# Reordering background work of a time-mix and GELU feed-forward kernel: copies first, an earlier first mix, weight terms in block 0

## The chip, the cores and the metric

One core of a Trainium2 chip. The metric is device time in microseconds, the median of repeated executions of the same program; lower is better.

## The reference

The input `x` is (4, 1024, 512) in f32. It is normalized over its last axis, goes through two branches, and both results are added to `x`.

```python
xn = _layernorm(x, axis=-1)
# attention-like branch, HIDDEN = 704
xx = concatenate([xn[:, 1:2], xn[:, :-1]], axis=1) - xn      # neighbour minus now
k = einsum('btc,hc->bth', xn + xx * time_mix_k, Wk)
r = einsum('btc,hc->bth', xn + xx * time_mix_r, Wr)
w = exp(-exp(time_decay))
state_t = state_{t-1} * w + relu(k_t);  out_t = state_t * r_t     # scan over the 1024 tokens
out = layernorm(einsum('bth,ch->btc', out, Wv)) * ln_gamma + ln_beta
# feed-forward branch, 2048 hidden
D = gelu(fp16(xn) @ W0.T + bias0).astype(fp16)
E = (D @ W1.T + bias1).astype(fp16)
return x + out + E
```

## The kernel before, in words

The tokens are cut into eight **blocks** of 512: `i` is the block at work, `j = i + 1` the next one. Even blocks begin a sequence, odd ones carry on from the state of the one before. All products run on TensorE in a reduced f32 format; for exactness operands are split into terms by VectorE and ScalarE. `split_x` makes three terms h, l, m of an x chunk, `split_kr` three terms of one tile of Wk or Wr (`kind` 0 is k, 1 is r), `split_w0`, `load_w1` and `split_wv` do so for the other weights. Terms that later blocks need are stored to DRAM (`krd`, `w0d`, `w1d`) and loaded from there (`load_kr`, `load_w1`, `load_w0l`).

A block is a loop over 16 **chunks** `n` of the feed-forward's hidden axis. In a chunk TensorE runs 8 matmuls of the up product (`up`, line 786, for the chunk two ahead), 8 of the down product (`down`, line 808, four accumulators `pe`, one for each 128 tokens) and then one **piece** of the attention branch: `raw_k`, `raw_r` and `raw_halves` in block 0 (plain f32 weights), `three_pass` (lines 628 and 385) and `half_pass` in later blocks, `out_full`/`out_halves` or `out_three_pass` (lines 723 to 733) in chunks 12 to 15. A normal chunk with a three-pass piece has 28 matmuls, one with a piece of the output 33.

A piece returns a **follower**, a generator with the work that ScalarE and VectorE do on its result in the next chunk: a scaled copy of `pa` on ScalarE (line 640, for the output 737), VectorE's combination with `pb` (641, 738), then the scan, the gating or the normalization with the residual (`residual`, lines 705 to 716, where two GpSimd instructions at lines 299 and 300 make the reciprocal deviation). Beside it runs the chunk's **background** list `bg[n]`, filled by `put`: loading, normalizing and transposing the next block's x (`turn`, line 331), its fp16 copies (`x16`), the scaled copies `scaled_now` (line 351), `mixed` (365 and 369) with the split of xk, and in the first two blocks the weight splits. `woven` alternates one step of each follower with one step of the background list. The order on TensorE, VectorE, ScalarE and the SP queue is exactly the order in which this code issues.

At the end of a block `rounded` empties the four `pe` banks on VectorE (line 765); the next block's down product takes the same four banks. Other buffers: four banks "mm" for all other products, six scratch tiles "s" (`temp`), six tiles "kr" (two weight tiles of three terms), two "w1", and 62 tiles "q" for everything that lives longer, raw weights among them. In block 0 the raw r weights are read by `raw_r` and stay in "q" until block 1 splits them.

In block 0, followers are finished at once, and `load_w1` for the chunk two ahead splits raw weights at the end of a chunk, after the background list; `store_weights` then issues the stores that the chunk has gathered on SP.

Of the kernel before, what the change touches and what calls it, by code (L numbers as in the profile page):

```python
# [22 lines left out]
def time_mix_and_gelu_ffn(  # L23
# [257 lines left out]
    def split_x(raw, name):  # L281
        u = truncated(raw, f"u{name}")
        h, l, m = (part(f"{p}{name}") for p in "hlm")
        nc.scalar.copy(h, u)  # L284
        yield
        nc.vector.tensor_sub(l, raw, u)
        yield
        nc.vector.scalar_tensor_tensor(m, l.bitcast(F32), -S, u, ALU.mult, ALU.add)
        return h, l, m
# [65 lines left out]
    def mixed(i, c):  # L355
        t0 = blocks[i][1]
        prior, now = xnT[:, c, :TB], xnT[:, c, 1:]
        if t0 > 0:
            nc.gpsimd.tensor_copy(xnT[:, c, 0:1], last[:, c, :])
        else:  # L360
            nc.vector.tensor_copy(xnT[:, c, 0:1], now[:, 0:2][:, 1:2])
        if t0 + TB < T:
            nc.gpsimd.tensor_copy(last[:, c, :], xnT[:, c, TB : TB + 1])
        xk, xr = parts_now.pop((i, c))
        nc.vector.scalar_tensor_tensor(
            xk, prior, mk_sb[:, c : c + 1], xk, ALU.mult, ALU.add
        )
        yield
        nc.vector.scalar_tensor_tensor(  # L369
            prior, prior, mr_sb[:, c : c + 1], xr, ALU.mult, ALU.add  # L370
        )
        xks[i, c] = yield from split_x(xk, f"k_{i}_{c}")
        xrs[i, c] = prior

    def split_xr(i, c):
        xrs[i, c] = yield from split_x(xrs[i, c], f"r_{i}_{c}")
# [127 lines left out]
    def woven(works, jobs):  # L504
        def steps():
            for job in jobs:
                yield from job() or ()
                yield

        others = steps()  # L510
        while works:
            works = [w for w in works if next(w, works) is None]
            next(others, None)
        finished(others)


# [187 lines left out]
    def residual(i, s, po):  # L704
        mv = small([P, 1, 2], "mv1", f"mvy_{i}_{s}", 4)
        stats_of(mv, 0, po, f"sty_{i}_{s}")
        rstd = rstd_of(mv[:, :, 1], f"ry_{i}_{s}")
        z = zs[i][:, s, :]
        y = temp(f"o_{i}_{s}") if i < RAW_OUT else po
        nc.vector.scalar_tensor_tensor(  # L710
            y, po, mv[:, 0, 0:1], gamma_sb, ALU.subtract, ALU.mult
        )

        yield
        nc.vector.scalar_tensor_tensor(y, y, rstd, beta_sb, ALU.mult, ALU.add)  # L715
        nc.vector.tensor_add(z, z, y)
# [152 lines left out]
    with tc.manual_schedule(engines=engines):  # L869
        for i in range(len(blocks)):  # L870
# [6 lines left out]
                bg[n].append(lambda: fn(*args))  # L877

            def fetch_kr(block, kind, h):
                if block == 1 and kind == 1:  # L880
                    ks[block, kind, h] = split_kr(kind, h)
                else:
                    ks[block, kind, h] = load_kr(block, kind, h)

            def fetch_x():
                state["x"] = load_x(j, "x")
# [12 lines left out]
            if i == 0:  # L899
                state["x"] = x_next  # L900
                pieces[1, 0] = [raw_k, i, 3]
                pieces[3, 0] = [raw_r, i, 3]
                pieces[5, 0] = [raw_k, i, 4]
                pieces[7, 0] = [raw_r, i, 4]
                pieces[9, 0] = [
                    lambda i: raw_halves(i, [bank(f"pkr_{i}_{q}") for q in range(2)]), i
                ]
                put(0, several, split_w0, (1, 2), (1, 3))
                for c in range(NC):
                    put(2 + c - (c == 0), split_w0, 2, c)  # L910
                    put(3 + c, load_w0, 3, c)
                    put(5 + c, split_w0, 3, c)
                put(1, stats, *range(NS))
                put(3, lambda: norm_apply(j, state["x"]))
                for h in range(NF):
                    put(1 + 2 * h, split_kr, 0, h)
                put(4, turn, 0, 1)
                put(5, turn, 1, 5)
                put(7, turn, 5, 10)
                put(8, turn, 10, 11)  # L920
                put(9, turn, 11, 16)
                put(4, load_late_constants)
                put(12, split_half)
                mix_at = (11, 12, 13, 15)
            else:
                order = [(0, h) for h in range(NF)] + [(1, h) for h in range(NF)]
                for k, (kind, h) in enumerate(order):
                    pieces[k + 2 * kind, 0] = [three_pass, i, kind, h]
                    if k > 1:
                        first = (5, 6, 8, 9, 10)[h] if i == kind == 1 else k - 2 + 2 * (k > 6)  # L930
                        put(first, fetch_kr, i, kind, h)
                pieces[5, 0] = [half_pass, i, 0]
                pieces[6, 0] = [half_pass, i, 1]
                for c, n in enumerate((1, 2, 3, 4) if i == 1 else (2, 2, 3, 3)):
                    put(n, split_xr, i, c)
                if j <= LAST:
                    put(2, fetch_x)
                    for s in range(NS):
                        put(4 + s // 2 if i == 1 else 4, stats, s)
                    put(6 if i == 1 else 5, lambda: norm_apply(j, state["x"]))  # L940
                    turns = (0, 5, 5, 5, 1) if i == 1 else (3, 4, 4, 3, 2)
                    for k in range(sum(turns)):
                        unit = next(n for n in range(5) if k < sum(turns[: n + 1]))
                        put(6 + unit, turn, k, k + 1)
                mix_at = (12, 13, 15, 15) if i == 1 else (12, 13, 14, 15)
            if i == 1:
                for g in range(NN // G):
                    put(2 * g, store_w0l, g)
                for h, n in enumerate((7, 10, 11, 12, 13, 13)):
                    put(n, split_wv, h)  # L950
            put(11 if j <= LAST else 2, fetch_residual)
            if j <= LAST:
                for c in range(NC):
                    put((10 if i == 0 else 11) + c // 2, x16, j, c)
                for c, n in enumerate(mix_at):
                    if n == mix_at[c - 1]:
                        put(n, scaled_now, j, c)
                    else:
                        early[n].append((j, c))
                    put(n, mixed, j, c)  # L960
                put(13, fetch_kr, j, 0, 0)
                put(14, fetch_kr, j, 0, 1)

            pe = [ps_e.tile([P, C], F32, tag="pe", name=f"pe_{i}_{s}") for s in range(NS)]
            for n in range(NN):
                ahead = n + AHEAD
                if ahead == NN and j <= LAST:
                    xf = next_xf
                nxt = (i, ahead) if ahead < NN else (j, ahead - NN)
                gelu = up(*nxt) if nxt[0] <= LAST else None  # L970
                several(scaled_now, *early[n])
                works = [follow() for follow in followers]
                if i == 0 or n == NN - NS or (n > NN - NS and i < RAW_OUT):
                    finished(*works)
                    works = []
                else:
                    works = [w for w in works if next(w, works) is None]
                followers = []
                if gelu:
                    d = gelu()  # L980
                if ahead + 1 == NN and j <= LAST:
                    next_xf = ffn_input(j)
                if n < NN - tail:
                    operands = waiting.pop(0)
                    for s in range(NS):
                        down(n, s, *operands, end=NN - tail if s in by_columns else NN)
                if gelu and i > 0:
                    waiting.append((d, load_w1(*nxt)))
                two_on = (i, ahead + 2) if ahead + 2 < NN else (j, ahead + 2 - NN)
                if two_on[0] <= LAST:  # L990
                    load_w0l(*two_on)
                jobs = [
                    lambda s=s: finish(i - 1, s, e16s[s])
                    for s in (2 * n, 2 * n + 1)
                    if s < len(e16s)
                ]
                for s in range(NS):
                    if (n, s) in pieces:
                        fn, *args = pieces[n, s]
                        followers.append(fn(*args))  # L1000
                if i == 0 and ahead + 1 < NN:
                    load_w1_raw(ahead + 1)
                woven(works, jobs + bg[n])
                if i == 0:
                    waiting.append((d, load_w1(*nxt)))
                store_weights()
# [60 lines left out]
```

## Time and profile before

| | us |
|---|---|
| median of 3 runs (889.73 to 890.12) | 889.89 |
| the profiled execution | 890.49 |
| its span, first to last instruction | 888.7 |
| TensorE busy | 867.3 (98%) |
| VectorE busy | 674.6 (76%) |
| ScalarE busy | 429.2 (48%) |
| GpSimd busy | 81.4 (9%) |
| moved by DMA | 195.01 MB, 219 GB/s on average |

Instructions are given as start, duration, engine, line of the source, operation and tiles out<-in. In brackets stands the engine's idle time before the instruction, and what ended it. Times are counted from the span's start. In the profile PE is TensorE, DVE VectorE, ACT ScalarE, POOL GpSimd, SP the queue that issues DMAs.

Blocks begin on TensorE at about 40, 136, 249, 355, 461, 568, 674 and 780 us.

### The profile page before, as it was taken

What the parts mean: (1) busy time and instruction counts of PE and PEld (TensorE: products, weight loads), DVE (VectorE), ACT (ScalarE), POOL (GpSimd) and SP (SyncE); (2) the same over time, 40 slices, a digit from 0 to 9 for tenths busy, and PEclk for the clock granted to TensorE, in tenths of its full rate; (3) what the DMA queues carried; (4) which work ended last, traced back from release to release, by engine and by line L of the source; (5) the groups of instructions that cost most, each with busy time, mean ns of one, the idle gap of its engine ahead of it and who ended that gap; (6) DMA issues with size and microseconds to landing.
All of it is one profiled execution on the core that took longest, in us unless ns stands there. A gap on an engine that the chain in (4) does not pass through costs nothing.

```text
span 888.7 us, 11076 instructions
## 1 busy us (share of the span) xinstructions
PE 867.3 (98%) x3760; PEld 687.3 (77%) x3760; DVE 674.6 (76%) x1098; ACT 429.2 (48%) x733; POOL 81.4 (9%) x142
## 2 busy tenths in 40 slices
PE   8999999999999999999999999999999999999996
PEld 7676658777578887888878888788887888878885
DVE  4767867598887878878788777878788786884547
ACT  3855734346634365443635446344463445444430
POOL 1100000000011001000021001100011200200001
PEclk8999999999999999999999999999999999999999
DMA  9569746866458655876548666595654956558631
GB/s 264 199 232 333 244 162 224 282 213 217 162 198 303 222 181 177 276 246 240 178 146 317 224 211 201 170 343 199 224 188 159 342 197 224 178 193 299 241 120 48
DMA packets 100164, 195.01 MB, mean 219 GB/s; under 512 B 10991, under 2 KB 25356, under 8 KB 100108
## 3 DMA queue, kind: packets, MB, share of 16 engines
q1 hardware_dynamic: 100048, 194.29, 64.0%
q8 instruction: 30, 0.49, 0.2%
q14 instruction: 26, 0.21, 0.1%
q10 hardware_dynamic: 60, 0.02, 0.0%
HBM read 165.43 MB, written 28.84 MB: 219 GB/s over the span
## 4 chain that ended last, share of the span: by engine, by line
PE 80%; DVE 11%; ACT 4%; POOL 2%; issue 2%; DVEq 0%; ACTq 0%
PE pd L786 22%; PE pe L808 22%; PE pa L628 13%; PE pb L385 7%; PE po L684 4%; PE oa L723 3%; PE ph L657 2%; PE pk L385 2%; PE pr L385 2%; PE ob L731 1%; POOL ry L300 1%; DVE oy L715 1%; DVE xnT L369 1%; DVE sty L305 1%; POOL ry L299 1%
## 5 line engine op out<-in xcount | busy, mean ns | idle before, releaser
L808 PE MATMUL pe<-w,d 128*128 128x512 f32 x1008 | 251.7, 392 | 6.6 <-DVE e L765 6.6
L808 PEld LDWEIGHTS pe<-w,d 128*128 128x128 f32 x1008 | 187.6, 188 | 51.2 <-DVE e L765 13.2
L786 PE MATMUL pd<-xf,w0h 128*128 128x512 f32 x512 | 204.4, 399 | 0.7 <-DVE y L641 0.7
L786 PE MATMUL pd<-xf,w0l 128*128 128x512 f32 x512 | 200.0, 391 | 0.0
L796 ACT ACTIVATE d<-pd,late_sb 128x512 f16<-128x512 f32 x128 | 87.7, 685 | 120.5 <-PE pd L786 120.2
L786 PEld LDWEIGHTS pd<-xf,w0h 128*128 128x128 f32 x512 | 96.7, 189 | 27.2 <-issue 5.7
L786 PEld LDWEIGHTS pd<-xf,w0l 128*128 128x128 f32 x512 | 96.6, 189 | 21.9 <-issue 1.9
L641 DVE SCALAR_TENSOR_TENSOR y<-pb,a 128x512 f32<-128x512 f32 x70 | 48.3, 690 | 63.8 <-PE pb L385 43.3
L640 ACT ACTIVATE a<-pa 128x512 f32<-128x512 f32 x70 | 41.8, 597 | 86.4 <-PE pa L628 86.4
L801 ACT CAST d<-d 128x512 fp32r<-128x512 f16 x128 | 79.5, 621 | 4.1
L331 DVE STREAM_TRANSPOSE xnT<-x 32x512 f32<-32x512 f32 x112 | 78.6, 702 | 2.0
L299 POOL TENSOR_SCALAR ry<-mvy 128x1 f32<-128x1 f32 x32 | 19.8, 619 | 431.2 <-DVE mvy L306 431.2
L628 PE MATMUL pa<-hk,kr 128*128 128x512 f32 x140 | 54.5, 389 | 0.0
L628 PE MATMUL pa<-lk,kr 128*128 128x512 f32 x140 | 54.5, 389 | 0.0
L643 ACT ACTIVATE y<-y 128x512 f32<-128x512 f32 x35 | 22.1, 633 | 57.7 <-DVE y L641 57.7
L628 PE MATMUL pa<-hr,kr 128*128 128x512 f32 x120 | 46.7, 389 | 0.0
L628 PE MATMUL pa<-lr,kr 128*128 128x512 f32 x120 | 46.7, 389 | 0.0
L723 PE MATMUL oa<-wv,hg 128*128 128x512 f32 x120 | 46.7, 389 | 0.0
L723 PE MATMUL oa<-wv,lg 128*128 128x512 f32 x120 | 46.7, 389 | 0.0
L284 ACT CAST hk<-uk 128x512 fp32r<-128x512 f32 x28 | 17.4, 621 | 56.9 <-DVE uk L235 56.9
L385 PE MATMUL pb<-mk,kr 128*128 128x512 f32 x140 | 37.4, 389 | 0.0
L521 DVE TENSOR_TENSOR_SCAN g<-late_sb,carry,y 128x512 f32<-128x512 f32 x20 | 25.7, 1284 | 14.1 <-ACT y L643 14.1
(166 smaller groups left out, 1359.6 us busy)
## 6 DMA issues: line engine op xcount, KB each, us to landing
w<-w1d SPq DMA_DIRECT2D x110, 512.0 KB, 3.6
kr<-krd SPq DMA_DIRECT2D x195, 256.0 KB, 4.9
w0l<-w0d SPq DMA_DIRECT2D x96, 256.0 KB, 4.1
x<-in_L_attn_x SPq DMA_DIRECT2D x32, 256.0 KB, 6.0
w1d<-w SPq DMA_DIRECT2D x16, 512.0 KB, 3.4
xres<-in_L_attn_x SPq DMA_DIRECT2D x32, 256.0 KB, 5.4
krd<-wt SPq DMA_DIRECT2D x30, 256.0 KB, 2.4
out<-xres SPq DMA_DIRECT2D x28, 256.0 KB, 3.9
```

The lines of the kernel that those rows point to most:

```text
L299: nc.gpsimd.tensor_scalar_add(r, var, EPS)
L331: nc.vector.transpose(dst[i * Q : (i + 1) * Q, :, :, j, :], src[j * Q : (j + 1) * Q, :, :, i, :],)
L385: return nc.tensor.matmul(dst, w[:, c, :], src, start=(c == 0), stop=(c == NC - 1))
L628: nc.tensor.matmul(pa, w[p][:, c, :], xs[j, c][p], start=(c == 0 and p == 0), stop=(c == NC - 1 and p == 1),)
L640: nc.scalar.activation(a, pa, AF.Copy, scale=1.0 + 1.0 / S)
L641: nc.vector.scalar_tensor_tensor(y, pb, -1.0 / S, a, ALU.mult, ALU.add)
L684: nc.tensor.matmul(pos[s], gs[i, h][:, s * P : (s + 1) * P], wv_raw[h], start=(h == 0), stop=False,)
L723: nc.tensor.matmul(pa, gs[i, h][p][:, cols], wv[h][p], start=(h == 0 and p == 0), stop=(h == NF - 1 and p == 1),)
L786: nc.tensor.matmul(pd, w, xf[c], start=(c == 0 and p == 0), stop=(c == NC - 1 and p == 1),)
L796: nc.scalar.activation(d16, pd, AF.Gelu, bias=b0_sb[:, n : n + 1])
L801: nc.scalar.copy(d, d16)
L808: nc.tensor.matmul(pe[s] if sum_ is None else sum_, d[:, s * P : (s + 1) * P], w1[p][:, cols], start=(n == first and p == 0), stop=(n == e ...
```

## The change

It has four parts, all of them of order:

- In a chunk, the first step of each follower, which holds the ScalarE copy of the piece, is issued ahead of `scaled_now` instead of behind it. `woven` starts with a background step instead of a follower's. `residual` has one more `yield` from block 2 on, after the GpSimd instructions.
- The split of xk leaves `mixed` and becomes a job of its own, `split_xk`. From block 1 on the first x chunk is mixed in chunk 10 and split in 11; the others follow in 12, 13, 15 (block 1) or 12, 13, 14. Transposes end with chunk 9 instead of 10, and `x16` begins in chunk 10. No two mixes share a chunk any more.
- `split_kr` for the r weights runs in block 0 (chunks 1, 3, 5, 7, 11), and block 1 loads those terms from DRAM in chunks 3, 4, 7, 8, 9, as later blocks do.
- In block 1 `split_xr` is one chunk later (2 to 5), and the first of the `split_wv` are moved from 7 and 10 to 9 and 11.

```diff
-        xks[i, c] = yield from split_x(xk, f"k_{i}_{c}")
-        xrs[i, c] = prior
+        xks[i, c], xrs[i, c] = xk, prior
+
+    def split_xk(i, c):
+        xks[i, c] = yield from split_x(xks[i, c], f"k_{i}_{c}")
...
         while works:
+            next(others, None)
             works = [w for w in works if next(w, works) is None]
-            next(others, None)
...
         rstd = rstd_of(mv[:, :, 1], f"ry_{i}_{s}")
+        if i >= RAW_OUT:
+            yield
...
             def fetch_kr(block, kind, h):
-                if block == 1 and kind == 1:
-                    ks[block, kind, h] = split_kr(kind, h)
-                else:
-                    ks[block, kind, h] = load_kr(block, kind, h)
+                ks[block, kind, h] = load_kr(block, kind, h)
...
                     put(1 + 2 * h, split_kr, 0, h)
+                    put((1, 3, 5, 7, 11)[h], split_kr, 1, h)
...
-                        first = (5, 6, 8, 9, 10)[h] if i == kind == 1 else k - 2 + 2 * (k > 6)
-                        put(first, fetch_kr, i, kind, h)
+                        put(k - 2 + 2 * (k > 6), fetch_kr, i, kind, h)
...
-                for c, n in enumerate((1, 2, 3, 4) if i == 1 else (2, 2, 3, 3)):
+                for c, n in enumerate((2, 3, 4, 5) if i == 1 else (2, 2, 3, 3)):
                     put(n, split_xr, i, c)
...
-                    turns = (0, 5, 5, 5, 1) if i == 1 else (3, 4, 4, 3, 2)
+                    turns = (1, 6, 6, 3) if i == 1 else (4, 5, 4, 3)
...
-                mix_at = (12, 13, 15, 15) if i == 1 else (12, 13, 14, 15)
+                mix_at = (10, 12, 13, 15) if i == 1 else (10, 12, 13, 14)
...
-                for h, n in enumerate((7, 10, 11, 12, 13, 13)):
+                for h, n in enumerate((9, 11, 11, 12, 13, 13)):
                     put(n, split_wv, h)
...
-                    put((10 if i == 0 else 11) + c // 2, x16, j, c)
+                    put((10, 10, 11, 12)[c], x16, j, c)
                 for c, n in enumerate(mix_at):
-                    if n == mix_at[c - 1]:
-                        put(n, scaled_now, j, c)
-                    else:
-                        early[n].append((j, c))
+                    early[n].append((j, c))
                     put(n, mixed, j, c)
+                    put(n + (n == 10), split_xk, j, c)
...
+                works = [follow() for follow in followers]
+                works = [w for w in works if next(w, works) is None]
                 several(scaled_now, *early[n])
-                works = [follow() for follow in followers]
                 if i == 0 or n == NN - NS or (n > NN - NS and i < RAW_OUT):
                     finished(*works)
                     works = []
-                else:
-                    works = [w for w in works if next(w, works) is None]
```

More of the change, by code (lines that the diff above doesn't have):

```diff
@@ L940, in time_mix_and_gelu_ffn @@
                     put(6 if i == 1 else 5, lambda: norm_apply(j, state["x"]))
-                    turns = (0, 5, 5, 5, 1) if i == 1 else (3, 4, 4, 3, 2)
+                    turns = (1, 6, 6, 3) if i == 1 else (4, 5, 4, 3)
                     for k in range(sum(turns)):
-                        unit = next(n for n in range(5) if k < sum(turns[: n + 1]))
+                        unit = next(n for n in range(4) if k < sum(turns[: n + 1]))
                         put(6 + unit, turn, k, k + 1)
-                mix_at = (12, 13, 15, 15) if i == 1 else (12, 13, 14, 15)
+                mix_at = (10, 12, 13, 15) if i == 1 else (10, 12, 13, 14)
             if i == 1:
```

## The prediction, made before the change was run

> **What bounds the kernel now.** I read the page's busy table first, then TensorE's waits, then the chain of waits and the timelines around each long wait. TensorE is busy 98% of the span, and no part of the change adds or removes a matmul. So the change can only act through the moments in which TensorE stands still, and the list of its waits is short.
>
> ```profile
> PE 867.3 (98%) x3760; PEld 687.3 (77%) x3760; DVE 674.6 (76%) x1098; ACT 429.2 (48%) x733; POOL 81.4 (9%) x142
> ```
> ```profile
> PE pe L808 <- DVE e L765: 6.6, 5, 1.8
> PE small L460 <- issue: 2.8, 1, 2.8
> PE pb L385 <- ACT a L640: 2.0, 1, 2.0
> PE idle L403 <- PEq L1050: 0.8, 1, 0.8
> PE pd L786 <- DVE y L641: 0.7, 1, 0.7
> ```
>
> Columns: who waits for whom, us in total, times, longest. Five waits are the starts of blocks 3 to 7: the first down matmul needs a bank of `pe`, which VectorE empties by L765. The other two are in block 1. L460 and L403 are the program's start, which the change leaves alone.
>
> Now the end of block 2 on VectorE:
>
> ```profile
> 346.69 0.69 DVE L738 SCALAR_TENSOR_TENSOR oy<-ob,oa 128x512 f32<-128x512 f32 x1 [0.95 <-ACT oa L737]
> ...
> 351.63 0.75 DVE L369 SCALAR_TENSOR_TENSOR xnT<-xnT,mix_sb,xr 128x512 f32<-128x512 f32 x1
> 352.30 0.42 DVE L235 TENSOR_SCALAR uk<-xk 128x512 int32<-128x512 int32 x1
> 352.75 0.69 DVE L286 TENSOR_TENSOR lk<-xk,uk 128x512 fp32r<-128x512 f32 x1
> 353.48 0.69 DVE L288 SCALAR_TENSOR_TENSOR mk<-lk,uk 128x512 fp32r<-128x512 f32 x1
> 354.09 2.48 DVE L765 TENSOR_TENSOR e<-pe,b_sb 128x512 f16<-128x512 f32 x4
> ```
>
> The evictions stand behind the mix and split of the fourth x chunk, made in chunk 15. TensorE's last up matmul begins at 353.4, the first down at 354.83. From the first up matmul of the last chunk to the next block's first L628 the timeline has 5.37 us (351.83 to 357.20), against 3.62 in mid-block (309.22 to 312.84): 1.75 lost. The five ends lose 1.74, 2.49, 1.74, 2.50, 1.74, **10.2 us**; odd blocks lose more.
>
> Block 1:
>
> ```profile
> 165.30 0.69 DVE L288 SCALAR_TENSOR_TENSOR mr<-lr,ur 128x512 fp32r<-128x512 f32 x1 [8.22 <-PE pb L385]
> ```
> ```profile
> 192.00:195.00 3.00, 3.00 (x9) 2.31 (x8) 2.87 (x6) 2.28 (x5) 0.00 (x0) 0.51 0.09 35
> ```
>
> VectorE stood 8.2 us before writing `mr` until a matmul that reads the third part of xk. I read this as a full pool "q": 5 of its 62 tiles still hold the raw r weights, and the tile that comes free is an `mk`. The backlog that follows makes TensorE wait at 166 (L641 late) and at 191 (a weight split ahead of the copy L640 on ScalarE). The second line (PE, PEld, DVE, ACT, POOL busy, granted clock, DMA share, GB/s) shows the clock at half after the second wait. L628 to the next piece's first matmul takes 7.34 us at 163.07 and 10.25 at 187.64, against 6.35 for a normal chunk: 0.99 + 3.90, **4.9 us**.
>
> **What the Trainium skill says.** "Perfetto Trace Analysis", Optimization Strategy, says to find the gaps of the saturated engine and the semaphore that ends each; that is what the wait list does here. "TensorE: Matmul & The Clock Gate", What's actually happening, gives half clock after an idle window of about 3.4 us. This trace agrees in kind, but a 2.0 us wait was enough at 191. Its section Architectural detail says that ScalarE and VectorE run strictly in order, as the evictions behind L288 show. "DMA: Bandwidth & Descriptors", Bandwidth, puts HBM transfers near 358 GB/s per core; this trace has 401 GB/s from 73 to 83 us at a full DMA share (1.04).
>
> **The change, part by part.**
>
> Blocks 2 to 6: the mixes move from chunks 12, 13, 14, 15 to 10, 12, 13, 14 (the first one's split to 11), the transposes from 3, 4, 4, 3, 2 in chunks 6 to 10 to 4, 5, 4, 3 in 6 to 9. One mix and split is L365, L369, L235, L286, L288: 0.67 + 0.67 + 0.45 + 0.73 + 0.61 from start to start, 3.1 us. Without it chunk 15 has L738, L305, L306, L710, L715, L716: 3.8 us and about 1 us of waiting for POOL's `ry` (L299 0.79 and L300 0.94 on the chain). L738 no longer waits for L737, because the copy now goes ahead of the two L351 (0.62 each). It can start at about 344.5, so the evictions run from about 349.5 to 352; TensorE wants the first bank at 353.64. Slack for the first bank is over 3 us: I take the whole 10.2 us (bounds 6 and 10.2). What would be late next is nothing on this path.
>
> The chunks that receive work, by VectorE's durations: chunk 7 gets five transposes (3.6) beside 2.5 of the half r piece, 6.1 of 6.35 us; chunk 8 keeps 3.3 + 2.9; chunk 10 has 3.3 + 1.4; chunk 11 3.3 + 1.8; chunks 13 and 14 3.8 + 3.1 of 7.48, as before. Nothing overflows, so I price these at nothing. The cover is each chunk's matmuls; if it is gone, L641 comes late and the next up matmul lacks a bank, as at 166 (bounds 0 and 2 us). The background job ahead of the follower fills the 0.70 us that the scan waits for L643; the new yield puts work where L715 waits 0.46 for POOL. Both shorten VectorE's queue, not TensorE's. ScalarE's scaled copies and the x16 casts only move; it is idle half the time. SP's queue is passed by no load in these blocks.
>
> Block 1 loses five splits: each L235 + L243 + L247 (0.45 + 0.73 + 0.60, 1.8 us of VectorE), L245 + L246 (1.2 of ScalarE), and three 256 KB stores; it gains 15 loads of the same size, in chunks 3, 4, 7, 8, 9. These wait on SP for the slot that the piece two chunks before frees, with the w1 load queued behind, the rhythm that blocks 2 to 6 have without a stall. `split_xr` is a chunk later, and the five raw tiles are gone. Both waits of block 1 should go: 4.9 us (bounds 2 and 4.9).
>
> Block 0 receives those splits in chunks 1, 3, 5, 7, 11: 9 us of VectorE, 6 of ScalarE, 15 stores on SP (3.9 MB, at 401 GB/s 9.8 us of DMA). In a chunk the new split stands ahead of the transposes and of the split of w1 for two chunks later (`load_w1`), which the down matmuls wait for. Before, that split ended tightly:
>
> ```profile
> 82.61 3.57 DVE L331 STREAM_TRANSPOSE xnT<-x 32x512 f32<-32x512 f32 x5
> 86.20 0.69 DVE L170 TENSOR_TENSOR w<-w1raw,w 128x512 fp32r<-128x512 f32 x1
> ```
>
> down(9) starts at 86.70, so its w1 comes with no slack (the waits have 0.3 us there). down(7) had about 2, down(3) 1.7, down(8) 4.
>
> - Chunks 1 and 3 add 1.8 each, within the slack of down(3) and of down(5) at 65.3 (w1 ready 62.2).
> - Chunk 5: ScalarE comes 1.2 late and the split adds 1.8. w1(7), ready at 74.1 before, comes at about 76.9; down(7) at 76.0 loses 0.75.
> - SP: the w1(5) store, late constants (ten transfers, 64 to 70) and w1raw(8) follow the stores of chunk 3, so w1raw(8) goes out about 3.4 late and lands at 81 instead of 77.7. ScalarE waits for it, and VectorE reaches chunk 7's first w0 difference at 83.3 instead of 80.1.
> - Chunk 7: 3.3 of backlog + 1.8. w1(9) is ready at about 91.8 instead of 86.8; TensorE, 0.75 late, loses 4.2 more.
> - That wait is longer than the one at 191, so I add the half clock that followed there: 3.90 less its wait, about 1.7.
>
> Later chunks shift with TensorE; chunk 11's split has 4.5 of slack at down(13). Block 0 loses 0.75 + 4.25 + 1.7 = **6.7 us** (bounds 1 and 10: the lower if ScalarE and VectorE overlap better, the upper if the `kr` slots, all six now filled in one chunk, wait for their stores in a full DMA queue).
>
> The last block and its tail keep their matmuls and VectorE's row of work: 0.
>
> Sum, against the profiled execution's 890.49 (span 888.7 and 1.8 around it): 890.49 - 10.2 - 4.9 + 6.7 = 882.1. The median is 889.89, 0.6 lower: **881.5**.
>
> **The rivals.**
>
> B: block 0 hides the splits. VectorE is busy 72% from 53 to 73 us (7.2 and 7.3 of 10), which speaks for it; the absent slack at down(9) speaks against. A loss under 3 us gives 889.9 - 15.1 + 0 to 3, 875 to 878.
>
> C, slower: stores and splits in block 0 feed each other. SP runs in order, so late splits hold w1raw loads, late loads hold ScalarE, and the six `kr` slots hold the next splits. If the DMA time of all 15 stores (9.8) and the 5 us of VectorE lateness add up, with half clock after two stalls (3.4), the loss is 18: 892.9. It decides from 15.1 us on. For it: DMA share 0.98 and 1.04 from 63 to 83. Against: before 53 and after 83 us there is room, and 6 of the 15 stores fall after 83.
>
> D: a new wait takes the place of the old ones in chunks 7 to 14 (a bank freed late, a temp of the six in "s"). One of 1 us in each of five blocks, on top of block 0's loss, gives 886.5; 2 us each with a 2 us loss at the ends gives 893.
>
> E: the mixes in chunk 15 are not what holds the evictions. The timeline contradicts it: L765 follows L288 by 0.6 us. Then 892.
>
> **How the numbers follow.** My forecast (block 0 loses 3 to 10, 878 to 885) has 0.60; B 0.13; D 0.14, of which 0.10 is still faster, 0.02 level and 0.02 slower; C and E 0.13, of which 0.02 is level. About 0.2% (1.8 us) is what a measurement of this kernel can tell from no change. Faster 0.60 + 0.13 + 0.10 = 0.83, same 0.04, slower 0.13. The range 876.5 to 888 leaves out the lower half of B and the slower cases.
>
> **What would show it.** Right: no wait of L808 on L765; `mr` without a long wait; L808 waiting for w1 (L170) near 87 to 92 with half clock after it. Wrong: waits on L765 that remain, a new bank wait between 40% and 90% of a block, or block 0 with more than 15 us of waits.

## The result, and the profile after

| | before | after |
|---|---|---|
| median of four runs each, us | 889.81 (888.66 to 890.12) | **882.32** (881.3 to 882.43) |
| span of the profiled execution, us | 888.7 | 880.6 |

The ratio is 0.9916, with a 95% interval of 0.9898 to 0.9933: 0.8% faster, where 881.5 was predicted. Three parts of the program moved. I read each from the starts of the same matmuls in both traces: a place from which after is later than it was is a loss, the other way a gain. down(n) is the down product of chunk n, w1(n) are its weights. **Half clock** is a stretch in which TensorE is granted half of its clock.

| place | predicted, us | measured, us |
|---|---|---|
| block 0, piece behind down(7), at 77.8 | +0.75 | +1.0 |
| block 0, down(9) to the next up, 86.7 to 92.4 | +5.95 | +6.2, of which 4.2 are two waits |
| block 1, at 166 | -1.0 | -1.0 |
| block 1, at 191 to 196 | -3.9 | -3.9 |
| five block ends | -10.2 | -10.3 |

The sum of the right column is -8.0; the span is 8.1 shorter.

The page of after, busy line, and then TensorE's waits in after (who waits for whom, us in total, times, longest):

```profile
PE 863.9 (98%) x3760; PEld 688.5 (78%) x3760; DVE 670.4 (76%) x1098; ACT 431.9 (49%) x733; POOL 73.9 (8%) x142
```
```profile
PE pe L812 <- DVE w L170: 3.1, 2, 2.4
PE small L462 <- issue: 2.2, 1, 2.2
PE pe L812 <- ACT w L169: 1.9, 1, 1.9
PE idle L405 <- PEq L1048: 0.8, 1, 0.8
PE pt L429 <- DVE x L309: 0.6, 1, 0.6
```

As many matmuls as before, and every engine's instruction count is unchanged. The five waits for VectorE's evictions are gone, and so are both of block 1. In their place the down product (808 before, 812 now) waits three times for a w1 split, by L169 on ScalarE and L170 on VectorE, all in block 0. The rest, L462, L405 and L429, is the program's start: TensorE leaves it 0.3 us later than in before. Single executions differ there; those of the experiments leave it between 0.2 us later and 1.6 us earlier.

The end of block 2 on VectorE, after (start, duration, line; L738 is now L742, L765 is L769):

```profile
347.19 0.69 DVE L742 SCALAR_TENSOR_TENSOR oy<-ob,oa 128x512 f32<-128x512 f32 x1 [0.74 <-PE ob L737]
...
351.18 0.69 DVE L720 TENSOR_TENSOR xres<-xres,oy 128x512 f32<-128x512 f32 x1
351.79 2.48 DVE L769 TENSOR_TENSOR e<-pe,b_sb 128x512 f16<-128x512 f32 x4
```

No mix stands between the residual and the evictions, and the first down of the next block starts at 356.21, 4.4 us behind the start of the evictions. Block 0 in after, first on ScalarE, then on VectorE in chunk 7:

```profile
81.53 0.62 ACT L169 CAST w<-w1raw 128x512 fp32r<-128x512 f32 x1 [5.10 <-DMA w1raw<-in_L_ffn_W]
```
```profile
84.23 0.69 DVE L170 TENSOR_TENSOR w0l<-w0raw,w0h 128x512 fp32r<-128x512 f32 x1 [1.36 <-ACT w0h L169]
...
88.54 3.57 DVE L331 STREAM_TRANSPOSE xnT<-x 32x512 f32<-32x512 f32 x5
92.13 0.69 DVE L170 TENSOR_TENSOR w<-w1raw,w 128x512 fp32r<-128x512 f32 x1
```

And two windows there in after (length; busy us of PE, PEld, DVE, ACT, POOL; granted clock, DMA share, GB/s):

```profile
89.00:93.00 4.00, 0.62 (x2) 0.31 (x3) 3.91 (x7) 3.55 (x6) 0.00 (x0) 1.00 1.04 406
93.00:97.00 4.00, 4.00 (x15) 2.19 (x19) 3.87 (x7) 1.66 (x3) 0.00 (x0) 0.57 0.99 384
```

The load of w1raw comes at 81.5 after 5.1 us of waiting, VectorE starts chunk 7 at 84.2, and the split that down(9) needs, made at 86.20 before, is made at 92.13. TensorE is nearly empty from 89 to 93, and from 93 to 97 its granted clock is 0.57 on average.

### The profile page after: what moved, and what is told of

Its sections match the earlier page's. It is cut to its first block, busy times and chain, and to the rows that moved or that the text cites. A ratio compares the mean times of both kernels' runs of the same rounds, so it can differ in the third digit from the quotient of the medians.

```text
span 880.6 us, 11149 instructions
## 1 busy us (share of the span) xinstructions
PE 863.9 (98%) x3760; PEld 688.5 (78%) x3760; DVE 670.4 (76%) x1098; ACT 431.9 (49%) x733; POOL 73.9 (8%) x142
## 4 chain that ended last, share of the span: by engine, by line
PE 93%; DMA 3%; DVE 3%; issue 1%; SPq 0%; ACT 0%; DVEq 0%; ACTq 0%
PE pd L790 25%; PE pe L812 24%; PE pa L630 14%; PE pb L387 7%; PE oa L727 6%; PE po L686 4%; PE ob L735 3%; PE ph L659 3%; PE pk L387 2%; PE ob L737 1%; DMA w0raw<-in_L_ffn_W 1%; PE pr L387 1%; DMA wvraw<-in_L_attn_Wv 1%; PE pkr L604 0%; PE po L698 0%
## 5 line engine op out<-in xcount | busy, mean ns | idle before, releaser
L812 PEld LDWEIGHTS pe<-w,d 128*128 128x128 f32 x1008 | 189.5, 188 | 45.6 <-DVE w L170 4.0
L630 PE MATMUL pa<-hr,kr 128*128 128x512 f32 x140 | 54.5, 389 | 0.0
L630 PE MATMUL pa<-lr,kr 128*128 128x512 f32 x140 | 54.5, 389 | 0.0
L299 POOL TENSOR_SCALAR ry<-mvy 128x1 f32<-128x1 f32 x32 | 16.5, 516 | 438.2 <-DVE mvy L306 438.2
L387 PE MATMUL pb<-mr,kr 128*128 128x512 f32 x140 | 37.4, 389 | 0.0
L686 PE MATMUL po<-wvraw,g 128*128 128x512 f32 x80 | 35.6, 592 | 0.0
```

What stands on the lines that cost most here:

```text
L387: return nc.tensor.matmul(dst, w[:, c, :], src, start=(c == 0), stop=(c == NC - 1))
L630: nc.tensor.matmul(pa, w[p][:, c, :], xs[j, c][p], start=(c == 0 and p == 0), stop=(c == NC - 1 and p == 1),)
L686: nc.tensor.matmul(pos[s], gs[i, h][:, s * P : (s + 1) * P], wv_raw[h], start=(h == 0), stop=False,)
L812: nc.tensor.matmul(pe[s] if sum_ is None else sum_, d[:, s * P : (s + 1) * P], w1[p][:, cols], start=(n == first and p == 0), stop=(n == e ...
```

## The experiments

Two theories compete. The prediction's: each part of the change has its own effect, moved mixes free the ends, the weight splits free block 1 and cost block 0. The rival: the parts overlap, so that one gain is had by several of them, and the weight splits may cost more than they bring. All kernels compute the whole reference. Those from before:

| kernel (edit made in before) | median, us | ratio, 95% | block 0 | block 1 | ends |
|---|---|---|---|---|---|
| e_mix: moved mixes, blocks 2 to 6 | 879.5 | 0.9883 (0.9868 to 0.9898) | 0 | 0 | -10.3 |
| e_weights: r splits in block 0 | 892.34 | 1.0026 (1.0015 to 1.0036) | +6.4 | -4.8 | +2.9 |
| e_copy: copy first | 879.41 | 0.9888 (0.9871 to 0.9905) | 0 | -0.7 | -10.3 |
| e_woven: background first, and the yield | 877.34 | 0.986 (0.9845 to 0.9874) | 0 | -2.9 | -10.3 |
| e_order: e_copy and e_woven | 876.82 | 0.9854 (0.984 to 0.9869) | 0 | -2.9 | -10.3 |
| e_late: e_mix and e_order | 876.2 | 0.9848 (0.9831 to 0.9864) | 0 | -2.9 | -10.3 |

The last three columns, in us, are read from the matmul starts, as above, against before's trace; changes of 0.2 us and less are written as 0. A ratio is taken against runs of before made together with the kernel's own (medians 889.82 to 890.06).

### The mixes alone: e_mix

```diff
-        xks[i, c] = yield from split_x(xk, f"k_{i}_{c}")
-        xrs[i, c] = prior
+        xks[i, c], xrs[i, c] = xk, prior
+
+    def split_xk(i, c):
+        xks[i, c] = yield from split_x(xks[i, c], f"k_{i}_{c}")
...
-                    turns = (0, 5, 5, 5, 1) if i == 1 else (3, 4, 4, 3, 2)
+                    turns = (0, 5, 5, 5, 1) if i == 1 else (4, 5, 4, 3, 0)
...
-                mix_at = (12, 13, 15, 15) if i == 1 else (12, 13, 14, 15)
+                mix_at = (12, 13, 15, 15) if i == 1 else (10, 12, 13, 14)
...
-                    put((10 if i == 0 else 11) + c // 2, x16, j, c)
+                    put((10, 10, 11, 12)[c] if i > 1 else (10 if i == 0 else 11) + c // 2, x16, j, c)
...
+                    put(n + (n == 10), split_xk, j, c)
```

> The kernel before, with only the moves of the mixes in blocks 2 to 6 (mixes in chunks 10, 12, 13, 14, first split in 11, transposes 4, 5, 4, 3 from chunk 6, x16 from chunk 10); followers' order, block 0 and block 1 as before. My theory: the chunk 15 work ahead of the evictions was the whole cause of the five waits, so they all go, 10.2 us: about 879.6 us, no wait of L808 on L765. Rival (the order of copies and followers is needed too, because L738 stays late): part of the waits stays, 882 to 886.

It measured 879.5. TensorE's waits of e_mix, without those of the start:

```profile
PE pb L387 <- ACT a L642: 2.0, 1, 2.0
...
PE pd L788 <- DVE y L643: 0.7, 1, 0.7
```

The five end waits are gone, both of block 1 are there as before. So the moved mixes alone bring the whole gain at the ends.

### The weights alone: e_weights

```diff
-                if block == 1 and kind == 1:
-                    ks[block, kind, h] = split_kr(kind, h)
-                else:
-                    ks[block, kind, h] = load_kr(block, kind, h)
+                ks[block, kind, h] = load_kr(block, kind, h)
...
+                    put((1, 3, 5, 7, 11)[h], split_kr, 1, h)
...
-                        first = (5, 6, 8, 9, 10)[h] if i == kind == 1 else k - 2 + 2 * (k > 6)
-                        put(first, fetch_kr, i, kind, h)
+                        put(k - 2 + 2 * (k > 6), fetch_kr, i, kind, h)
```

> The kernel before, with only the splits of the r weights moved to block 0 and loaded in block 1. My theory: block 0 loses the 7.2 us that the changed kernel shows there, block 1 gains most of its 4.9, the five ends stay: about 892 us, slower than before. Rival (block 1's waits come from split_xr and split_wv being early, not from the raw tiles): they stay, 897.

It measured 892.34, slower than before by 0.26%. TensorE's waits of e_weights:

```profile
PE pe L808 <- DVE e L765: 6.6, 5, 1.8
PE pe L808 <- DVE w L170: 2.8, 2, 2.1
...
PE pe L808 <- ACT w L169: 1.4, 1, 1.4
```

The ends stay, block 1 is free, block 0 has the three waits of after. Block 0 costs 6.4 and block 1 returns 4.8, so this part of the change is a loss by itself. The 2.9 at the ends came with the clock: two of the five waits, which end at 462 and 677 us, were followed by half clock here and not in before (1.3 and 1.5 us). They belong to this one execution, the slowest of eight (893.76); the median is 2.3 above that of before, near the 1.6 that blocks 0 and 1 give together.

### The order alone, and with the mixes: e_order, e_late

```diff
         while works:
-            works = [w for w in works if next(w, works) is None]
             next(others, None)
+            works = [w for w in works if next(w, works) is None]
...
         rstd = rstd_of(mv[:, :, 1], f"ry_{i}_{s}")
+        if i >= RAW_OUT:
+            yield
...
-                several(scaled_now, *early[n])
                 works = [follow() for follow in followers]
+                works = [w for w in works if next(w, works) is None]
+                several(scaled_now, *early[n])
...
-                else:
-                    works = [w for w in works if next(w, works) is None]
```

> The kernel before, with only the order inside a chunk changed: the follower's first step ahead of the scaled copies, a background step first in woven, the yield after the GpSimd instructions. The mixes stay in chunks 12 to 15. My theory: in chunk 15 L738 starts about 1 us earlier and the 0.46 us wait for POOL is filled, so each end loses 1.5 us less of its 1.75 or 2.5: about 883 us. Rival (VectorE's row of work in chunk 15 is what is too long, whatever its order): the five waits stay at 10 us, 889.5.

> Both of these together: all that the change does to blocks 2 to 6, with the weight splits and the mixes of blocks 0 and 1 as before. My theory: the ends lose nothing, 10.2 us, and block 1 keeps its two waits (4.9): 879.6 us, faster than the change as a whole by 2.7. Rival (the new order also removes block 1's waits): 875 to 877.

e_order measured 876.82, 6 us under what was expected, with the mix still in chunk 15. Its end of block 2 on VectorE:

```profile
340.72 0.69 DVE L740 SCALAR_TENSOR_TENSOR oy<-ob,oa 128x512 f32<-128x512 f32 x1 [1.08 <-PE ob L735]
...
346.44 0.68 DVE L288 SCALAR_TENSOR_TENSOR mk<-lk,uk 128x512 fp32r<-128x512 f32 x1
347.04 2.48 DVE L767 TENSOR_TENSOR e<-pe,b_sb 128x512 f16<-128x512 f32 x4
```

The evictions follow L288 as closely as in before, and are early nevertheless: chunk 15 began at 340.44, so L740 starts 0.3 us into it. In before it starts 2.3 in. And e_order is rid of the wait at 191 as well, with the raw r weights still in the pool "q". e_late, 876.2, adds nothing that can be told from e_order: the two gains at the ends are the same gain. Its rival, that the order also frees block 1, held for the wait at 191; the one at 166 stays.

### Each half of the order: e_copy, e_woven

e_copy has the last part of the diff above (from `several` on), e_woven the first two, each alone.

> The kernel before, with only the follower's first step (the ScalarE copy of the piece and VectorE's combination) issued ahead of the scaled copies; woven and residual as before. My theory: the late L738 (2.3 us into chunk 15, against 0.3 where the order is changed) is the larger part of each end's lateness, so the five waits shrink from 1.75 and 2.5 to under 0.6 each, and the 191 wait of block 1 stays, since its copy stood behind a weight split and not behind scaled copies: 881 to 883 us. Rival (the alternation does it): 888 or above.

> The kernel before, with only woven begun by a background step and the extra yield in residual; the copies stay behind the scaled copies. My theory: it fills only the 0.46 us before L715 in each of the output's chunks, so the ends keep 1 us or more each, but in block 1 background splits get ahead and the 191 wait goes (3.9 us): about 882. Rival (the alternation is what removes the ends' waits): 877 or below.

Both freed all five ends: e_copy as its theory had it, if more fully, e_woven as its rival had it. That each alone would do it was not foreseen. The cause can be read on VectorE in before, in the chunks ahead of the end of block 2. Here are steps of L738 in before, then in e_copy:

```profile
329.82 0.69 DVE L738 SCALAR_TENSOR_TENSOR oy<-ob,oa 128x512 f32<-128x512 f32 x1 [0.95 <-ACT oa L737]
...
338.25 0.69 DVE L738 SCALAR_TENSOR_TENSOR oy<-ob,oa 128x512 f32<-128x512 f32 x1 [0.95 <-ACT oa L737]
```
```profile
328.13 0.69 DVE L738 SCALAR_TENSOR_TENSOR oy<-ob,oa 128x512 f32<-128x512 f32 x1 [0.84 <-PE ob L733]
...
335.62 0.69 DVE L738 SCALAR_TENSOR_TENSOR oy<-ob,oa 128x512 f32<-128x512 f32 x1
...
343.10 0.69 DVE L738 SCALAR_TENSOR_TENSOR oy<-ob,oa 128x512 f32<-128x512 f32 x1
```

In before the steps are 8.43 apart (and 8.44 to the one at 346.69, shown in the prediction), while TensorE's chunk with an output piece takes 7.48: VectorE falls 0.95 us behind in every chunk. In e_copy they are 7.49 and 7.48 apart. The 0.95 is just the wait for L737; it stands ahead of L738 in chunks 14 and 15 of blocks 2 to 6 alike. ScalarE in before shows why it is late:

```profile
344.31 0.62 ACT L284 CAST hk<-uk 128x512 fp32r<-128x512 f32 x1 [4.03 <-DVE uk L235]
344.84 0.72 ACT L351 ACTIVATE xk<-xnT,rest_sb 128x512 f32<-128x512 f32 x1
345.47 0.71 ACT L351 ACTIVATE xr<-xnT,rest_sb 128x512 f32<-128x512 f32 x1
346.08 0.57 ACT L737 ACTIVATE oa<-oa 128x512 f32<-128x512 f32 x1
```

This is a ring. VectorE's L235 of one chunk, late in its list, lets ScalarE make `hk`; behind that stand the two L351 and then the copy L737; and on the copy waits VectorE's next L738, which stands ahead of everything else that VectorE has to do in the next chunk. ScalarE was idle for 4.03 us, and the ring turns in 8.44. VectorE's own work in a turn is 8.44 - 0.95 - 0.46 (for `ry`) = 7.03, less than TensorE's 7.48. Nothing is too long; the two lists wait for one another. That ScalarE runs strictly in order (the Trainium skill, "TensorE: Matmul & The Clock Gate", Architectural detail) is what makes the L351 count, and these four rows agree: L737 starts at 346.08, 1.7 us into chunk 15 (which starts at 344.35). In after the same copy, with nothing ahead of it, starts 1.4 us before chunk 15 does (345.53 against 346.92). By that, it could have started at 343.0 in before.

Each edit meets it at another place. e_copy takes the L351 out of the ring. e_woven leaves L738 waiting for the copy, but brings VectorE's L235 forward, from 5.6 to 2.7 us behind L738 (343.86 - 338.25 in before, 337.33 - 334.61 in e_woven), and the ring turns in 7.35. e_mix keeps one slow turn, and L738 starts 1.3 us into chunk 15; what it takes away is the mix behind it. The evictions' start, counted from the first up matmul of chunk 15 in block 2:

| kernel | chunk 15 starts | evictions start | into the chunk |
|---|---|---|---|
| before | 344.35 | 354.09 | 9.74 |
| e_copy | 342.82 | 350.49 | 7.67 |
| e_woven | 341.79 | 348.39 | 6.60 |
| e_order | 340.44 | 347.04 | 6.60 |
| e_mix | 344.27 | 350.14 | 5.87 |
| after | 346.92 | 351.79 | 4.87 |

TensorE wants the first bank 9.29 into the chunk (356.21 - 346.92 in after), and needs 0.74 from the start of the evictions (354.83 - 354.09 in before), so 8.55 is early enough. Before misses it by 1.2 (and loses 1.75 in all, as the next banks come late too); all others meet it. That is why the gains don't add.

The wait at 191 is of the same kind. In before, ScalarE's copy L640 stands behind a weight split that waits 5.44 us for VectorE:

```profile
189.72 0.62 ACT L266 CAST wv<-vu 128x512 fp32r<-128x512 f32 x1 [5.44 <-DVE vu L235]
190.44 0.63 ACT L267 ACTIVATE wv<-vd 128x512 fp32r<-128x512 f32 x1
190.98 0.58 ACT L640 ACTIVATE a<-pa 128x512 f32<-128x512 f32 x1
```

e_copy leaves it, since no L351 is issued in those chunks and so nothing changes place there; e_woven moves VectorE's steps, so that VectorE comes to this L235 at 187.35 instead of 189.25, and the wait is gone. TensorE's waits of e_copy, then of e_woven:

```profile
PE pb L385 <- ACT a L640: 2.7, 2, 2.0
...
PE pd L786 <- DVE y L641: 0.7, 1, 0.7
```
```profile
PE pd L788 <- DVE y L641: 0.7, 1, 0.7
PE pb L385 <- ACT a L640: 0.6, 1, 0.6
```

What stays in e_woven is the wait at 166, and there is a new one of 0.6 at 212, which costs 0.9. e_copy has it too (0.7), so the new order is not needed for it. In e_copy the wait at 191 is as long as in before, but no half clock follows:

```profile
190.70:194.10 3.40, 3.38 (x15) 2.81 (x16) 3.27 (x6) 2.67 (x5) 0.00 (x0) 1.00 0.08 31
```

TensorE gains 1.6 us by that. It starts the last matmul ahead of the place at 212 some 2.5 us earlier than in before (209.67 against 212.16), while the copy L640 that it needs next starts only 0.9 earlier (210.09 against 210.97). So the half clock of before hid a wait; with the r splits out of block 1, in e_weights and after, there is none at that place.

### The pool: e_hold

From after, the raw r tiles are held until block 1 by copies of one column, whose result is not used, in chunks 5, 6, 8, 9 and 10, and `split_xr` goes back to chunks 1 to 4.

```diff
     def split_kr(kind, h):
         raw = raw_w.pop((kind, h)).rearrange("p c k -> p (c k)")
+        held[kind, h] = raw
...
-                for c, n in enumerate((2, 3, 4, 5) if i == 1 else (2, 2, 3, 3)):
+                for c, n in enumerate((1, 2, 3, 4) if i == 1 else (2, 2, 3, 3)):
...
+                for h, n in enumerate((5, 6, 8, 9, 10)):
+                    put(n, touch, h)
```

> The changed kernel, with the five raw r weights kept in their tiles until chunks 5, 6, 8, 9, 10 of block 1 (a one-column copy there reads each once more, its result unused) and split_xr in chunks 1 to 4 as before: the same splits as in the changed kernel, the same pressure on the tiles q as before. My theory (a full pool q): VectorE waits about 8 us before a write of mr again, until the pieces' matmuls read the mk, and TensorE loses about 1 us near 173: 883.3. Rival (the split work in block 1 was the cause): no such wait, 882.3.

It measured 882.06 (ratio 0.9921, 0.9901 to 0.9941); the medians can't tell this from after. The traces can: block 1 loses 1.0 again at 166, and this execution happens to lose 0.6 less in block 0. VectorE in e_hold, and its TensorE waits:

```profile
171.58 0.69 DVE L295 SCALAR_TENSOR_TENSOR mr<-lr,ur 128x512 fp32r<-128x512 f32 x1 [8.22 <-PE pb L394]
```
```profile
PE pd L797 <- DVE y L650: 0.7, 1, 0.7
```

The 8.22 us are back to the hundredth, with the wait of 0.7 at 166 behind them, and no wait at 191. So the full pool is shown as the cause of the first wait only (held tiles and the earlier `split_xr` together; which of the two alone would do was not tried).

### Block 0: e_const, e_spread, e_both, e_best

Four versions of after. e_const issues the ten late constants in chunk 10 instead of 4. e_spread puts the r splits in chunks 1, 11, 11, 12, 12; e_both does both; e_best takes e_const with the splits in 1, 3, 6, 7, 11.

```diff
-                put(4, load_late_constants)
+                put(10, load_late_constants)
```
```diff
-                    put((1, 3, 5, 7, 11)[h], split_kr, 1, h)
+                    put((1, 11, 11, 12, 12)[h], split_kr, 1, h)
```

> The changed kernel, with the late constants (Wv, gamma, beta, bias1: ten transfers) loaded in chunk 10 of block 0 instead of chunk 4, so that fewer transfers stand ahead of w1raw(8). My theory: the 5.1 us that ScalarE waits for w1raw(8) go, chunk 7 starts at about 80 us again, w1(9) comes at 87.9 and down(9) loses 0.3 instead of 4.9 and the half clock: block 0 loses about 1.5 instead of 7.2, 876.5 us. Rival (VectorE's own 1.8 us a chunk is the cause and the queue only fills its slack): down(9) still loses 3 or more, 880 or above.

> The changed kernel, with the r splits of block 0 in chunks 1, 11, 11, 12, 12 instead of 1, 3, 5, 7, 11, behind the crowded stretch. My theory: down(7) and down(9) lose nothing, block 1's waits stay away, 7.2 us less: 875.3 us, faster than both. Rival (the splits only carry the wait along: w1(13) and the mixes of chunks 12 and 13 come late): a wait of 2 us or more between 103 and 135 us, 877 or above.

> Both: r splits in chunks 1, 11, 11, 12, 12 and the late constants in chunk 10. My theory: nothing is left in block 0 for the constants to free but 0.3 us at down(9): the same as with the splits moved alone, within 0.5 us. Rival (the constants' transfers in chunk 10 now stand ahead of w1raw(13) and (14)): 1 us or more slower.

> The changed kernel, with the late constants in chunk 10 and the third r split in chunk 6 instead of 5, so that w1(7) is no longer behind two weight splits in chunk 5. My theory: down(7) loses nothing more, 1.0 us less than with the constants moved alone: 874.5 us, the fastest here. Rival (w1(8), split at the end of chunk 6, now comes late for down(8), or the six kr tiles hold chunk 7's splits): 875.5 or above.

| kernel | median, us | ratio to before, 95% |
|---|---|---|
| after | 882.32 | 0.9916 (0.9898 to 0.9933) |
| **e_const** | **875.53** | 0.9836 (0.982 to 0.9853) |
| e_spread | 881.41 | 0.9905 (0.9889 to 0.9922) |
| e_both | 882.87 | 0.9921 (0.9905 to 0.9936) |
| e_best | 877.25 | 0.9864 (0.9848 to 0.9881) |

e_const is as expected (876.5). SP's queue in after, then in e_const, shows the load that ScalarE waits for:

```profile
67.66 2.38 SPq L159 DMA_DIRECT2D wvraw<-in_L_attn_Wv  x5
...
73.63 0.33 SPq L164 DMA_DIRECT2D b_sb<-in_L_ffn_bias  x1
74.35 0.33 SPq L204 DMA_DIRECT2D w1d<-w  x1
75.25 0.33 SPq L208 DMA_DIRECT2D w1raw<-in_L_ffn_W  x1
```
```profile
67.98 0.33 SPq L204 DMA_DIRECT2D w1d<-w  x1
68.36 0.43 SPq L208 DMA_DIRECT2D w1raw<-in_L_ffn_W  x1
```

Without the constants it is issued at 68.36 instead of 75.25, lands at 73.75 instead of 81.44, and the split for down(9) follows at 86.96 instead of 92.13 (VectorE in e_const):

```profile
86.96 0.69 DVE L170 TENSOR_TENSOR w<-w1raw,w 128x512 fp32r<-128x512 f32 x1
```

Of the three block 0 waits 0.7 us at down(7) is left, and no half clock. The same r splits of the same length stand in the same chunks: what cost the 6.2 at down(9) was transfers ahead of one load. The splits and their stores used up the slack: before has the constants in the same chunk and does not lose there.

e_spread takes away the early loss too, all but 1.3 us at down(9), but loses 6.0 late in block 0, as its rival had it, and ends up within a microsecond of after. TensorE's waits of e_spread and of e_best:

```profile
PE pd L790 <- ACT xf L383: 4.4, 1, 4.4
...
PE pe L812 <- DVE w L170: 1.1, 1, 1.1
```
```profile
PE pe L812 <- DVE w L170: 2.6, 1, 2.6
```

Late splits make ScalarE late with the copies `xf` for the next block's first up product. In e_both that wait is 6.4 us, and it is 1.5 slower than e_spread, as much as its rival had said, but not through the w1raw loads that the rival named. ScalarE stands before a weight split until the store of an earlier one has landed and its "kr" tile is free, 4.75 us against 0.69 in e_spread:

```profile
112.22 0.62 ACT L245 CAST wt<-wu 128x512 fp32r<-128x512 f32 x1 [4.75 <-DMA krd<-wt]
```

The constants now stand ahead of these stores on SP (94 to 100 us; the stores follow from 105).

In e_best the split moved from chunk 5 to 6 frees down(7) and comes too close to down(9), which loses 2.7. Of the three sets of places tried for the r splits with the constants in chunk 10, that of after is the best.

**The best version** is e_const, 875.53: faster than before by 1.6% and than after by 0.8%. e_late, without the weights' part, has a ratio (0.9848) that lies within its interval, so the two can't be told apart.

## Why the prediction was right, and where its reasons were not

- **The ends.** The size, 10.2, was right to 0.1, and so was the picture: L738 was expected at 344.5 and the evictions from 349.5; counted from the chunk's start in before, they came at 344.6 and 349.2. The reason was half of it. The prediction took the fourth mix in chunk 15 as what holds the evictions; e_copy and e_woven show that it may stay. To remove the lag that VectorE had gathered, 2.1 us at L738, was enough as well. The step that failed is the sentence that background first and the yield shorten VectorE's queue, not TensorE's: alone they bring the whole gain.
- **Block 1.** 4.9 was right, in part by luck: 1.6 us of it is half clock, which the same wait of 2.0 us in e_copy did not bring. That a full pool makes `mr` wait was right (e_hold). That the wait at 191 is its backlog was wrong: it goes with the order (e_woven) while the wait at 166 stays, goes with the weights' part (e_weights), and stays away when the pool's wait is back (e_hold). It is ScalarE's copy behind a split that waits for VectorE, and the edits that removed it changed what VectorE has to do ahead of that split.
- **Block 0.** 6.7 was predicted and 7.2 measured. The chain held link by link (predicted, then measured in brackets): w1raw at 81 (81.5), chunk 7's first w0 difference at 83.3 (84.2), w1(9) ready at 91.8 (92.8), then half clock. e_const confirms the late constants as the link that decides. The half clock was a guess from one wait, and it came. Down(7) was 0.25 under, down(9) 0.25 under; the 0.9 us by which chunk 7 came later than predicted is ScalarE, waiting 5.1 for the load and then starting with w0h at 83.6 (0.2 more for its own load).
- **The work moved into other chunks** was priced at nothing, and no wait appeared there.
- **The rivals.** B (block 0 hides the splits) was wrong for this order, though e_const at 875.5 is what B would have given. C and D did not occur in after, though e_both shows C's wait for the "kr" tiles. E was right in a way the prediction had not meant: the mixes can stay in chunk 15, and the gain came all the same. What the prediction held against E, that L765 follows L288 by 0.6 us, decides nothing: it does so in e_copy and e_order too (347.04 behind 346.44 in e_order), and no wait follows.
- The sum came out because the terms were measured as gaps in one trace, each regained or not; it did not depend on which edit regains it. As an account of the change it hides that, once the order is new, the weights' part and the moves in block 1 that go with it cost about 6 us: after minus e_late is 882.32 - 876.2, and the traces have 7.2 lost in block 0 against 2.0 more regained in block 1 (4.9 against 2.9).

## What to carry to other kernels

When two in-order engines wait for each other once in every step, compare the step's period on each engine with the bound engine's: an excess that equals an idle time points to a ring like this one, and here one reordering removed it without any change in the work. Test the parts of a change alone, since several may buy the same gain and one may eat it. When work moves to an earlier stage, look at the tightest load there and at what its own queue has ahead of it.

## What the runs showed of the hardware

- **Half clock came after waits much shorter than one window, but not always.** The Trainium skill ("TensorE: Matmul & The Clock Gate", What's actually happening) speaks of an idle window of about 3.4 us. Half clock followed the 2.0 us wait at 191 in before and e_mix, and did not follow the same 2.0 us wait in e_copy. It followed waits of 1.8 us at two of the five ends in e_weights; the same five ends in before had none. Where it followed one of these waits it lasted 3.4 us and cost 1.3 to 1.6. So what a short wait costs can't be read from its length. The same section calls the window free-running; that the place of a wait within it decides is my reading and not shown.
- **The DMA rate** was 406 GB/s over 4 us in after, at a full share (1.04), and 401 over 10 us in before. The skill ("DMA: Bandwidth & Descriptors", Bandwidth) gives about 358 GB/s for a core when both cores that share a memory stream, and more for one core alone; this program runs on one core. These windows mix loads and stores.
